# The last 64 keys of a slot in half-width values and quarter-array sums, and a new order of loads at the start, in a gated cross-attention block

## The chip, the cores and the metric

The kernel runs on one core of a Trainium2 chip (trn2). The metric is the device time of one execution in microseconds (us); lower is better. PE is TensorE, the matmul engine, PEld its weight loads; DVE is VectorE, ACT ScalarE, POOL GpSimd, SP SyncE. A line such as L891 is a line of the kernel before.

## The reference

One layer of a gated cross-attention block with a ternary feed-forward net. There are 16 batches, 224 rows of 512 in `x`, and 750 context keys of 384 in each; a mask leaves out part of the keys. There are 8 heads of 64, and gelu is the exact one.

```python
def attention(x, context, mask):          # x is layernormed first
    q = x @ W_q;  k = context @ W_k;  v = context @ W_v        # 8 heads of 64
    sim = einsum('bihd,bjhd->bhij', q, k) * 64 ** -0.5
    sim = where(mask[:, None, None, :], sim, -finfo.max)
    return einsum('bhij,bjhd->bihd', softmax(sim), v) @ W_o + b_o
def bitlinear(x, w, b):
    return act_quant(rmsnorm(x)) @ weight_quant(w).T + b       # 8 bits; -1, 0, 1
x = x + tanh(g_xattn[0]) * attention(layernorm(x), context, mask)
x = x + tanh(g_ffn[0]) * bitlinear(gelu(bitlinear(layernorm(x), w1, b1)), w2, b2)
```

`weight_quant` divides by the mean of |w| over the whole matrix, so no weight of w1 or w2 (each 1,048,576 values, 4.2 MB) can be rounded before all of them have been summed.

## The kernel before, in words

`order_batches` (L30) counts the keys that a batch attends to, sorts the batches by that count and gives each a slot. Slots 0 to 7 hold up to 192 keys, slots 8 to 15 up to 128 (`CAPS`). If all batches fit, `compact_path` (L709) runs, else `dense_path`; in the run shown it is `compact_path`. Only the kept keys are fetched, so a slot has one tile of 128 keys, and in slots 0 to 7 a second tile of 64, "the rest".

**One slot.** `select` (L797) builds six 0/1 masks on DVE (`ind`, L803), counts with them on PE which key goes to which place (`pi`, L810), and writes the key numbers and the mask for the scores (L819, L826). `gather` (L831) fetches these keys' context rows by an indirect DMA that POOL issues, 128 rows per tile, the second tile too. `context_pieces` (L854) turns the context on PE (`trans`, L867, six transposes of 128x128 in a slot with two tiles), makes the keys from it (`kp`, L876) and the values (`vp`, L891), one 128x512 projection of three matmuls for each tile. The second tile's values go into `v_rest`, a zeroed buffer of [128, 4, 2, 64] per parity of slot. Its 128 rows are the 64 keys twice: `place` repeats the numbers 128 to 191. Rows 0 to 63 hold the even head of a pair in the first 64 columns, rows 64 to 127 the odd head in the last 64, and the rest is zero, so that one full matmul adds the rest of both heads.

The x rows are fetched by `fetch` (L915), two tiles of 128 rows, layernormed by `norm` (L921: bn_stats and bn_aggr on DVE, then the power, the negated mean and the centring on POOL), turned (L951) and projected to queries (L972). `scores` (L1001) does, for four of the eight heads and half of the rows, four matmuls over 64 rows (L1011), the mask and minimum on DVE (L1025), exp on ACT (L1035), the reciprocal on DVE (L1044) and a multiply on POOL (L1045). `turn_probs` (L1055) transposes the probabilities into `pT`. `weighted` (L1079) sums them with the values: 16 half-width matmuls (64 output rows each) for the first tile (L1089), then, with a rest, four full ones with `v_rest` (L1100), all into two PSUM banks (index `a`); the heads of a pair lie in output rows 0 to 63 and 64 to 127. An fp32 matmul is two records of the trace.

**After attention**, pairs of 128-row tiles go through `residual` (L1134), `project` with `wo` (L1143, L1148), `normalise` (L1172), `up` (L1218), `gelu` (L1231) and `down` (L1264), with the FFN weights in fp8. These weights are made during slots 0 (w1) and 1 (w2): `load_weights` (L1299) brings eight chunks ("raw", 0.5 MB each), `sum_weights` (L1314) sums |w| on DVE and ACT by turns, `scale_weights` (L1329) adds up the sums with one PE matmul (`wtotp`), `round_weights` (L1350) rounds a chunk in three DVE passes into a bf16 tile of the tag `xq`, and `turn_weights` (L1359) turns it on PE. `evict` (L738) gives each copy out of PSUM to DVE or ACT, by running estimates of their load. PSUM has two wide tiles for scores, `av` and `hp`, and four banks for all else.

**Order.** Each slot is a loop pass (L1441): `merge` (L1389) interleaves three lists by their estimated costs in us: the attention of slot s, the preparation for later slots (`norm_pieces(s + 2)`, `gather(s + 2)`, `select(s + 3)`, context and queries of slot s + 1), and the weights (s < 2) or the FFN. Then the first two scores of slot s + 1 follow. Within that order a scheduler puts instructions into the engines' queues, each of which runs in order. Before the loop stands the start:

```python
    fetch(0)
    select(0)
    gather(0)
    norm(0, (0,))
    norm(0, (1,))
    fetch(1)
    select(1)
    gather(1)
    for piece in query_pieces(0) + context_pieces(0):
        piece[1]()
    fetch(2)
```

followed by `norm_pieces(1)`, `select(2)`, the eight loads of w1, `late_loads` (L220: b_o, b2, w_o and b1 on SP's queue, the biases broadcast to 128 partitions) and the first two scores of slot 0.

Of the kernel before, what the change touches and what calls it, by code (L numbers as in the profile page):

```python
# [29 lines left out]
def order_batches(ctx, tc, sh, mask, x, context):  # L30
# [44 lines left out]

    spread(spread_no, start, nc.gpsimd, nc.gpsimd)
# [15 lines left out]
    nc.gpsimd.tensor_copy(m, m8)  # L92

# [43 lines left out]
    nc.vector.tensor_copy(n_odd, odds)  # L137

# [19 lines left out]
def flamingo_gated_kernel(  # L158
# [61 lines left out]
    def late_loads():  # L220
        nc.sync.dma_start(sh.bo, b_o.partition_broadcast(P))
        nc.sync.dma_start(sh.b2, b2.partition_broadcast(P))
        nc.sync.dma_start(sh.wo, w_o.rearrange("(c p) i -> p c i", p=P))
        nc.sync.dma_start(sh.b1, b1.partition_broadcast(P))
# [4 lines left out]
    with few.Else():  # L229
        with ExitStack() as stage:  # L230
            late_loads()
# [477 lines left out]
def compact_path(ctx, tc, sh, x, context, out, late_loads):  # L709
# [74 lines left out]

    place = pa.tile([P, 256], BF16, name="place")
    numbers(place[:, :192], [[1, 192]], 0, 0)
    numbers(place[:, 192:], [[1, 64]], 128, 0)
    place_f = pa.tile([TQ, 320], BF16, name="place_f")
    numbers(place_f[:, :192], [[1, 192]], 0, 0)
    numbers(place_f[:, 192:], [[1, P]], 0, 0)  # L790
    first = pa.tile([P, B], F32, name="first")
    nc.gpsimd.tensor_scalar(first, sh.slots[:, 1, :], float(J), None, ALU.mult)

    live = [{} for _ in range(B + 1)]
    kctx = context.rearrange("b j c -> (b j) c")

    def select(s):  # L797

        st = live[s]
        nt = 2 if CAPS[s] > P else 1  # L800
        ind = pa.tile([TJ, NJ, 256], BF16, tag="ind", name=f"ind_{s}", bufs=1)
        for n in range(NJ):
            nc.vector.tensor_scalar(  # L803
                ind[:, n, : nt * P], place[:TJ, : nt * P], sh.upto[:, n, s : s + 1], None, ALU.is_ge
            )
        load["v"] += 6 * 200
        pi = gen([P, 2], F32, f"pi_{s}")
        for t in range(nt):
            for n in range(NJ):
                nc.tensor.matmul(  # L810
                    pi[:, t : t + 1],
                    lhsT=ind[:, n, t * P : (t + 1) * P],
# [6 lines left out]
        nc.vector.tensor_scalar(  # L819
            keys[:, :nt], pi[:, :nt], float(J - 1), first[:, s : s + 1], ALU.min, ALU.add  # L820
        )
# [5 lines left out]
            mb[:, :nm], place_f[:, :nm], sh.slots[:TQ, 0, s : s + 1], -FMAX, ALU.is_ge, ALU.mult  # L827
# [3 lines left out]
    def gather(s):  # L831
# [3 lines left out]
        for t in range(nt):  # L835
            nc.gpsimd.indirect_dma_start(
                out=kept[:, t, :],
                out_offset=None,
                in_=kctx,
                in_offset=bass.IndirectOffsetOnAxis(ap=st["keys"][:, t : t + 1], axis=0),  # L840
# [5 lines left out]


    v_rest = []
# [666 lines left out]
```

## Time and profile before

| what | value |
|---|---|
| time before, median of 3 runs | 785.88 us (785.7 to 787.6) |
| the profiled execution's own time | 788.52 us |
| its span, first to last instruction | 786.8 us |
| mean granted TensorE clock | 0.971 |
| busy PE / PEld / DVE / ACT / POOL | 696.5 / 448.0 / 508.5 / 392.1 / 367.7 us |
| DMA traffic | 59.53 MB in 87280 packets |
| vp (L891), both tiles, 144 records | 68.0 us |
| av of the rest (L1100), 64 records | 14.2 us |
| a chunk of w1 or w2 (0.5 MB), issue to landing | 4.9 us median |
| x tiles, issue to landing | 5.9 us median |

How to read the profile: a row of groups names the line, the engine, the operation, output and inputs, shapes and number of records, then the busy time in us, the mean ns of one, and the idle time just before them with what ended it. Records of matmuls overlap, so their means are longer than the distance between two of them. A row of busy time by stage gives the window, its length, busy us and records of PE, PEld, DVE, ACT and POOL, the granted clock, the DMA share and GB/s. A row of waits says which engine and line waited for which other engine and line, then total us, number of times and longest. The timeline gives start, length, engine, line and operation, and in brackets the idle time before it. The chain of waits follows the work that ended last back to the start.

### The profile page before, as it was taken

What the parts mean: (1) busy time and instruction counts of PE and PEld (TensorE: products, weight loads), DVE (VectorE), ACT (ScalarE), POOL (GpSimd) and SP (SyncE); (2) the same over time, 40 slices, a digit from 0 to 9 for tenths busy, and PEclk for the clock granted to TensorE, in tenths of its full rate; (3) what the DMA queues carried; (4) which work ended last, traced back from release to release, by engine and by line L of the source; (5) the groups of instructions that cost most, each with busy time, mean ns of one, the idle gap of its engine ahead of it and who ended that gap; (6) DMA issues with size and microseconds to landing.
All of it is one profiled execution on the core that took longest, in us unless ns stands there. A gap on an engine that the chain in (4) does not pass through costs nothing.

```text
span 786.8 us, 11011 instructions
## 1 busy us (share of the span) xinstructions
PE 696.5 (89%) x3790; PEld 448.0 (57%) x3790; DVE 508.5 (65%) x1281; ACT 392.1 (50%) x950; POOL 367.7 (47%) x478
## 2 busy tenths in 40 slices
PE   2588889899999899999989899989898999989762
PEld 2466666676566565665756476656574756543321
DVE  4366776667772955848568635575758577688960
ACT  0264937344563735628264674373737365455340
POOL 6834245746083451753728343655362525254331
PEclk9999999999999999999999989999999999999887
DMA  7913412101231401415032330141404031323331
GB/s 278 340 47 106 160 28 67 35 15 47 40 75 54 104 28 43 89 54 104 29 67 78 78 67 12 54 104 54 79 27 91 17 81 41 67 54 92 85 88 48
DMA packets 87280, 59.53 MB, mean 76 GB/s; under 512 B 75424, under 2 KB 75440, under 8 KB 87088
## 3 DMA queue, kind: packets, MB, share of 16 engines
q1 hardware_dynamic: 78960, 32.00, 17.6%
q0 software_dynamic: 8256, 26.75, 10.9%
q8 instruction: 32, 0.52, 0.3%
q14 instruction: 32, 0.26, 0.1%
HBM read 33.04 MB, written 7.34 MB: 51 GB/s over the span
## 4 chain that ended last, share of the span: by engine, by line
PE 63%; DVE 19%; ACT 5%; issue 4%; POOL 4%; DMA 2%; POOLq 0%; DVEq 0%; ACTq 0%; SPq 0%
PE qp L972 13%; PE fp L1264 10%; PE hp L1218 9%; PE vp L891 7%; PE kp L876 6%; PE op L1148 6%; DVE a L1241 5%; PE av L1089 3%; DVE h L1226 3%; PE ptp L1065 3%; PE sim L1011 3%; DVE hq L1244 2%; DVE ind L803 2%; PE av L1100 2%; DVE hq L1245 2%
## 5 line engine op out<-in xcount | busy, mean ns | idle before, releaser
L1045 POOL TENSOR_TENSOR p<-p,rec 112x768 f32<-112x768 f32 (+1 forms) x64 | 81.8, 1281 | 130.5 <-DVE rec L1044 61.7
L1226 DVE SCALAR_TENSOR_TENSOR h<-hp,c,b_bc 128x1024 f32<-128x1024 f32 x56 | 71.6, 1281 | 86.6 <-PE hp L1218 85.6
L1218 PE MATMUL hp<-w1T,xqT 128*128 128x512 fp8e4 x448 | 106.3, 384 | 8.9 <-DMA xqT<-xq 5.1
L1035 ACT ACTIVATE p<-p,nm 112x192 f32<-112x192 f32 (+1 forms) x256 | 106.7, 421 | 7.9 <-DVE nm L1025 7.0
L1264 PE MATMUL fp<-w2T,hqT 128*128 128x512 fp8e4 x448 | 103.7, 386 | 7.5 <-DMA hqT<-hq 7.5
L972 PE MATMUL qp<-xnT,wq_sb 128*128 128x224 f32 x512 | 106.4, 363 | 1.3 <-ACT xnT L747 1.1
L1148 PE MATMUL op<-wo_sb,xoT 128*128 128x512 f32 x224 | 106.2, 609 | 1.0 <-DVE keys L819 0.9
L972 PEld LDWEIGHTS qp<-xnT,wq_sb 128*128 128x128 f32 x512 | 98.7, 196 | 7.5 <-ACT xnT L747 1.9
L1025 DVE CUSTOM_DVE_ANT_0 p<-sim,mask 112x192 f32<-112x192 f32 (+1 forms) x256 | 70.3, 316 | 29.2 <-PE sim L1011 16.5
L1218 PEld LDWEIGHTS <-xqT 128*128 128x128 bf16 x448 | 43.8, 99 | 62.3 <-issue 13.8
L1241 DVE TENSOR_REDUCE a<-h 128x1 f32<-128x2048 f32 x28 | 63.9, 2281 | 22.6 <-ACT h L1238 22.6
L1264 PEld LDWEIGHTS <-hqT 128*128 128x128 bf16 x448 | 43.7, 99 | 59.6 <-DMA hqT<-hq 8.9
L1238 ACT ACTIVATE h<-h 128x2048 f32<-128x2048 f32 x28 | 53.5, 1912 | 42.2 <-DVE h L1226 24.4
L876 PE MATMUL kp<-ctxT,wk_sb 128*128 128x192 f32 (+1 forms) x384 | 65.5, 323 | 5.6 <-ACT xnT L747 3.6
L774 POOL DMA_INDIRECT x<-in_x_dram,token x28 | 33.1, 1182 | 77.2 <-PE ctxp L867 36.8
L891 PE MATMUL vp<-wv_sb,ctxT 128*128 128x512 f32 x144 | 68.0, 610 | 0.0
L876 PEld LDWEIGHTS kp<-ctxT,wk_sb 128*128 128x128 f32 x384 | 59.8, 207 | 13.3 <-ACT xnT L747 5.2
L747 ACT COPY qT<-qp 128x448 f32<-128x448 f32 x30 | 16.0, 532 | 94.8 <-PE qp L972 94.8
L1148 PEld LDWEIGHTS op<-wo_sb,xoT 128*128 128x128 f32 x224 | 40.4, 192 | 39.0 <-issue 35.6
L1011 PE MATMUL sim<-kT,qT 64*112 64x192 f32 (+1 forms) x512 | 55.2, 317 | 8.4 <-DVE nm L1025 7.4
L1250 ACT ACTIVATE sq<-h 128x2048 bf16<-128x2048 f32 x28 | 53.2, 1900 | 7.6 <-DMA hqT<-hq 3.9
L1011 PEld LDWEIGHTS sim<-kT,qT 64*112 64x112 f32 x512 | 37.9, 172 | 28.2 <-DVE nm L1025 11.6
(157 smaller groups left out, 1117.9 us busy)
## 6 DMA issues: line engine op xcount, KB each, us to landing
raw<-in_L_ffn_w_dram SPq DMA_DIRECT2D x16, 512.0 KB, 4.9
wq_sb<-in_L_xattn_W_q_dram SPq DMA_DIRECT2D x1, 1024.0 KB, 5.9
wo_sb<-in_L_xattn_W_o_dram SPq DMA_DIRECT2D x1, 1024.0 KB, 7.9
b_bc<-in_L_ffn_b_dram SPq DMA_DIRECT2D x1, 1024.0 KB, 11.1
wk_sb<-in_L_xattn_W_k_dram SPq DMA_DIRECT2D x1, 768.0 KB, 7.4
wv_sb<-in_L_xattn_W_v_dram SPq DMA_DIRECT2D x1, 768.0 KB, 8.9
x<-in_x_dram,token POOLq DMA_INDIRECT x28, 5.9
y<-in_x_dram,token POOLq DMA_INDIRECT x28, 3.4
```

Of the source, the lines that this page charges most:

```text
L876: nc.tensor.matmul(pk[:, p - p0, :], lhsT=sh.wk[:, c, p * P : (p + 1) * P], rhs=st["ctxT"][:, c, :cap], start=(c == 0), stop=(c == NC - 1),)
L891: nc.tensor.matmul(pv, lhsT=st["ctxT"][:, c, t * P : (t + 1) * P], rhs=sh.wv[:, c, :], start=(c == 0), stop=(c == NC - 1),)
L972: nc.tensor.matmul(pq[:, i, :], lhsT=sh.wq[:, d, (p + i) * P : (p + i + 1) * P], rhs=st["xnT"][:, d, :], start=(d == 0), stop=(d == ND - 1),)
L1011: nc.tensor.matmul(sim[:, j, i, :cap], lhsT=st["qT"][j * DH : (j + 1) * DH, p, q * TQ : (q + 1) * TQ], rhs=st["kT"][j * DH : (j + 1) * DH, ...
L1025: nc.vector.tensor_tensor_reduce(out=probs[:, h, :cap], in0=sim[:, j, i, :cap], in1=st["mask"][:, j * begin : j * begin + cap], scale=-(DH ...
L1035: nc.scalar.activation(probs[:, h, :cap], probs[:, h, :cap], AF.Exp, bias=nmax, scale=-1.0, accum_out=total[:TQ, h : h + 1],)
L1045: nc.gpsimd.tensor_tensor(probs[:, :, :cap], probs[:, :, :cap], rec[:TQ].unsqueeze(2).to_broadcast([TQ, 4, cap]), ALU.mult,)
L1148: nc.tensor.matmul(po, lhsT=xoT[:, d, at : at + P], rhs=sh.wo[:, d, :], start=(d == 0), stop=(d == ND - 1))
L1218: nc.tensor.matmul(ph[:, n, :], lhsT=f["xqT"][:, k * ND + d, :], rhs=w1T[:, d, at : at + NB], start=(d == 0), stop=(d == ND - 1),)
L1226: nc.vector.scalar_tensor_tensor(h[:, cols], ph.rearrange("t i n -> t (i n)"), f["c1", k], sh.b1[:, cols], ALU.mult, ALU.add)
L1241: nc.vector.tensor_reduce(amax[:, k : k + 1], h, AX.X, ALU.max, apply_absolute_value=True)
L1264: nc.tensor.matmul(po, lhsT=f["hqT", k][:, n, :], rhs=w2T[:, n, :], start=(n == 0), stop=(n == NF - 1))
```

## The change

What it does, in six parts:

- The rest is held once. `select` and `gather` handle 64 rows for the second tile (`rows_of`), `ctxT` is 192 wide, and the transposes of the second tile take 64 rows.
- The values of the rest (`values_rest`) are made in two halves of 64 output rows, even heads in rows 0 to 63 and odd heads in rows 64 to 127, each over 256 columns of `wv` read in runs of 64. `v_rest` becomes a dense rotating tile [128, 4, 64] that one copy fills; zeroed buffers and memsets go.
- In `weighted`, the rest is added by eight matmuls of 64 rows by 64 columns, and for `a` = 1 the two heads of a pair change places in the output rows (`a ^ j`). `late_loads` brings `wo` with the matching halves crossed.
- The number patterns `place`, `place_f` and `first` are made in `order_batches`, `first` on ACT.
- At the start, `norm_first` normalises each tile of x_0 by itself, with only the power on POOL; fetches of x_1 and x_2 and the gather of slot 1 are issued after that power, and the w1 loads right after the first of them. The w1 sums and scale come before the first scores; b_o, b1, b2 and the first half of `wo` get a one-element copy from the last sum, so that their loads wait for it.
- The w2 chunks are loaded and summed among the w1 rounding and turning (`weight_pieces`), the turn of a chunk comes two chunks after its rounding, and the `xq` tag has three buffers.

```diff
@@ order_batches @@
+    sh.place = const.tile([P, 192], BF16, name="place")
+    sh.place_f = const.tile([P, 320], BF16, name="place_f")
     spread(spread_no, start, nc.gpsimd, nc.gpsimd)
...
     nc.gpsimd.tensor_copy(m, m8)
+    numbers(sh.place, [[1, 192]], 0, 0)
+    numbers(sh.place_f[:, :192], [[1, 192]], 0, 0)
+    numbers(sh.place_f[:, 192:], [[1, P]], 0, 0)
...
     nc.vector.tensor_copy(n_odd, odds)
+
+    sh.first = const.tile([P, B], F32, name="first")
+    nc.scalar.activation(sh.first, sh.slots[:, 1, :], AF.Copy, scale=float(J))
@@ flamingo_gated_kernel @@
-    def late_loads():
+    def late_loads(crossed):
         nc.sync.dma_start(sh.bo, b_o.partition_broadcast(P))
         nc.sync.dma_start(sh.b2, b2.partition_broadcast(P))
-        nc.sync.dma_start(sh.wo, w_o.rearrange("(c p) i -> p c i", p=P))
+        by = w_o.rearrange("(c p) i -> p c i", p=P)
+        if crossed:
+
+            h = P // 2
+            nc.sync.dma_start(sh.wo[:, 0:2, :], by[:, 0:2, :])
+            nc.sync.dma_start(sh.wo[:h, 2:4, :], by[h:, 2:4, :])
+            nc.sync.dma_start(sh.wo[h:, 2:4, :], by[:h, 2:4, :])
+        else:
+            nc.sync.dma_start(sh.wo, by)
         nc.sync.dma_start(sh.b1, b1.partition_broadcast(P))
@@ compact_path @@
-    place = pa.tile([P, 256], BF16, name="place")
-    numbers(place[:, :192], [[1, 192]], 0, 0)
-    numbers(place[:, 192:], [[1, 64]], 128, 0)
-    place_f = pa.tile([TQ, 320], BF16, name="place_f")
-    numbers(place_f[:, :192], [[1, 192]], 0, 0)
-    numbers(place_f[:, 192:], [[1, P]], 0, 0)
-    first = pa.tile([P, B], F32, name="first")
-    nc.gpsimd.tensor_scalar(first, sh.slots[:, 1, :], float(J), None, ALU.mult)
-
+    def rows_of(s, t):
+        return min(CAPS[s] - t * P, P)
@@ select @@
-            nc.vector.tensor_scalar(
-                ind[:, n, : nt * P], place[:TJ, : nt * P], sh.upto[:, n, s : s + 1], None, ALU.is_ge
-            )
+            nc.vector.tensor_scalar(ind[:, n, :cap], sh.place[:TJ, :cap], sh.upto[:, n, s : s + 1], None, ALU.is_ge)
...
+            rows = rows_of(s, t)
             for n in range(NJ):
                 nc.tensor.matmul(
-                    pi[:, t : t + 1],
-                    lhsT=ind[:, n, t * P : (t + 1) * P],
+                    pi[:rows, t : t + 1],
+                    lhsT=ind[:, n, t * P : t * P + rows],
@@ after gather @@
-    v_rest = []
-    for i in range(2):
-        t = pa.tile([P, NP, 2, DH], F32, name=f"v_rest_{i}")
-        nc.gpsimd.memset(t, 0.0)
-        v_rest.append(t)
@@ context_pieces @@
             for c in range(c0, c1):
                 for t in range(nt):
+                    rows = rows_of(s, t)
                     nc.tensor.transpose(
-                        pt[:, c - c0, t * P : (t + 1) * P], st["ctx"][:, t, c * P : (c + 1) * P], ident
+                        pt[:, c - c0, t * P : t * P + rows],
+                        st["ctx"][:rows, t, c * P : (c + 1) * P],
+                        ident[:rows, :rows],
                     )
-            evict(st["ctxT"][:, c0:c1, : nt * P], pt, (c1 - c0) * nt * P)
+            evict(st["ctxT"][:, c0:c1, :cap], pt, (c1 - c0) * cap)
...
-        def values(t):
-            pv = gen([P, D], F32, f"vp_{s}_{t}")
+        def values():
+            pv = gen([P, D], F32, f"vp_{s}")
...
-            if t == 0:
-                evict(st["v"], pv, D)
-            else:
-                st["v_rest"] = v_rest[s % 2]
-                by = pv.rearrange("p (i j d) -> p i j d", j=2, d=DH)
+            evict(st["v"], pv, D)
+
+        def values_rest():
+
+            pv = gen([P, NP, DH], F32, f"vr_{s}")
+            for c in range(NC):
+                by = sh.wv[:, c, :].rearrange("p (i j d) -> p i j d", j=2, d=DH)
                 for j in range(2):
-                    rows = slice(j * DH, (j + 1) * DH)
-                    evict(st["v_rest"][rows, :, j, :], by[rows, :, j, :], D // 2)
+                    nc.tensor.matmul(
+                        pv[j * DH : (j + 1) * DH],
+                        lhsT=st["ctxT"][:, c, P:],
+                        rhs=by[:, :, j, :],
+                        start=(c == 0),
+                        stop=(c == NC - 1),
+                    )
+            st["v_rest"] = pa.tile([P, NP, DH], F32, tag="v_rest", name=f"v_rest_{s}", bufs=2)
+            evict(st["v_rest"], pv, D // 2)
@@ before slot_xnT @@
+    def norm_first(k):
+
+        xp = normed[0]
+        st = small(f"bs_x0_{k}", 6)
+        nc.vector.bn_stats(st, xp[:, k, :])
+        mv = small(f"mv_x0_{k}", 4)
+        nc.vector.bn_aggr(mv[:, :2], st)
+        rstd = small(f"rs_x0_{k}")
+        nc.vector.tensor_scalar(rstd[:, :1], mv[:, 1:2], EPS, None, ALU.add)
+        power = nc.gpsimd.tensor_tensor(rstd[:, :1], rstd[:, :1], sh.mhalf[:, :1], ALU.pow)
+        nc.vector.tensor_scalar(xp[:, k, :], xp[:, k, :], mv[:, 0:1], rstd[:, :1], ALU.subtract, ALU.mult)
+        return power.ins
@@ weighted @@
+                    rows = slice((a ^ j) * DH, ((a ^ j) + 1) * DH)
                     nc.tensor.matmul(
-                        by[j * DH : (j + 1) * DH, a, i, :],
+                        by[rows, a, i, :],
...
         if rest:
-            for a in range(2):
-                for i in range(2):
+
+            for i in range(2):
+                for a in range(2):
                     p = 2 * a + i
-                    nc.tensor.matmul(
-                        by[:, a, i, :],
-                        lhsT=st["v_rest"][:, p].rearrange("p j d -> p (j d)"),
-                        rhs=st["pT"][:, 8 + p, :],
-                        start=False,
-                        stop=(i == 1),
-                    )
+                    for j in range(2):
+                        keys = slice(j * DH, (j + 1) * DH)
+                        rows = slice((a ^ j) * DH, ((a ^ j) + 1) * DH)
+                        nc.tensor.matmul(
+                            by[rows, a, i, :],
+                            lhsT=st["v_rest"][keys, p, :],
+                            rhs=st["pT"][keys, 8 + p, :],
+                            start=False,
+                            stop=(i == 1),
+                        )
@@ normalise and round_weights @@
-            f["xq"] = pa.tile([P, 2, D], BF16, tag="xq", name=f"xq_{i}", bufs=2)
-            f["xqT"] = pa.tile([P, 2 * ND, P], BF16, tag="xq", name=f"xqT_{i}", bufs=2)
+            f["xq"] = pa.tile([P, 2, D], BF16, tag="xq", name=f"xq_{i}", bufs=3)
+            f["xqT"] = pa.tile([P, 2 * ND, P], BF16, tag="xq", name=f"xqT_{i}", bufs=3)
...
-        quantised[wi, c] = w16 = pa.tile([P, W], BF16, tag="xq", name=f"w16_{wi}_{c}", bufs=2)
+        quantised[wi, c] = w16 = pa.tile([P, W], BF16, tag="xq", name=f"w16_{wi}_{c}", bufs=3)
@@ weight_pieces @@
         p = []
         if wi == 1:
-            p += [(0.0, lambda c=c: load_weights(wi, c)) for c in range(NPC)]
-        p += [(0.4, lambda c=c: sum_weights(wi, c)) for c in range(NPC)]
-        p += [(0.1, lambda: scale_weights(wi))]
-        for c in range(NPC + 1):
+            p += [(0.0, lambda: scale_weights(1))]
+        for c in range(NPC + 2):
             if c < NPC:
-                p += [(0.0, lambda c=c: round_weights(wi, c))]
-            if c > 0:
-                p += [(0.6, lambda c=c: turn_weights(wi, c - 1))]
+                p += [(0.2, lambda c=c: round_weights(wi, c))]
+                if wi == 0:
+                    p += [(0.0, lambda c=c: load_weights(1, c))]
+            if c > 1:
+                p += [(0.6, lambda c=c: turn_weights(wi, c - 2))]
+                if wi == 0:
+                    p += [(0.0, lambda c=c: sum_weights(1, c - 2))]
         return p
@@ the start, after the functions of compact_path @@
     fetch(0)
     select(0)
     gather(0)
-    norm(0, (0,))
-    norm(0, (1,))
-    fetch(1)
     select(1)
-    gather(1)
+    norm_first(0)
+    with tc.issue_after(norm_first(1)):
+        fetch(1)
+        gather(1)
+        fetch(2)
+    late["stage"] = ExitStack()
+    late["raw"] = late["stage"].enter_context(tc.tile_pool(name="raw", bufs=1))
+    with tc.issue_after(load_weights(0, 0)):
+        for c in range(1, NPC):
+            load_weights(0, c)
     for piece in query_pieces(0) + context_pieces(0):
         piece[1]()
-    fetch(2)
     for _, piece in norm_pieces(1):
         piece()
     select(2)
-    late["stage"] = ExitStack()
-    late["raw"] = late["stage"].enter_context(tc.tile_pool(name="raw", bufs=1))
     for c in range(NPC):
-        load_weights(0, c)
-    late_loads()
+        sum_weights(0, c)
+    scale_weights(0)
+
+    for dst in (sh.wo[0:1, 0, 0:1], sh.bo[0:1, 0:1], sh.b1[0:1, 0:1], sh.b2[0:1, 0:1]):
+        nc.scalar.copy(dst, weight_sums[0][0:1, NPC - 1 : NPC])
+    late_loads(True)
     scores(0, 0)
     scores(0, 1)
```

## The prediction

> **What bounds the kernel now.** I read the page first, then busy time by stage, then who PE waited for, then the timeline of the start and of one slot.
>
> ```profile
> PE 696.5 (89%) x3790; PEld 448.0 (57%) x3790; DVE 508.5 (65%) x1281; ACT 392.1 (50%) x950; POOL 367.7 (47%) x478
> ...
> PE 63%; DVE 19%; ACT 5%; issue 4%; POOL 4%; DMA 2%; POOLq 0%; DVEq 0%; ACTq 0%; SPq 0%
> ```
>
> PE leads both in busy time and in the chain that ended last. By stage (length, then busy PE, PEld, DVE, ACT, POOL):
>
> ```profile
> 20.00:40.00 20.00, 10.85 (x46) 9.44 (x46) 6.38 (x15) 4.97 (x11) 15.60 (x21) 1.00 0.94 335
> ...
> 60.00:80.00 20.00, 15.81 (x100) 12.48 (x100) 14.46 (x37) 9.15 (x24) 7.01 (x9) 0.91 0.37 120
> ...
> 300.00:350.00 50.00, 49.17 (x251) 30.91 (x249) 33.39 (x78) 26.71 (x63) 24.55 (x31) 1.00 0.26 63
> ```
>
> There are three regimes. Until about 30 us PE hardly works while DMA is full (0.94). In slots 0 and 1 (to about 130 us) PE has holes. From there to 430 us it is busy 49 of 50 us, DVE 33: work taken from PE there is time. PE's longest wait and what stands behind it:
>
> ```profile
> PE xnp L951 <- POOL x L938: 14.4, 2, 12.9
> ```
>
> ```profile
> 12.09 1.25 POOL L774 DMA_INDIRECT x<-in_x_dram,token  x1 [0.18 <-issue]
> ...
> 25.94 0.77 POOL L938 TENSOR_SCALAR x<-x,ls_x,rs_x 128x512 f32<-128x512 f32 x1
> ...
> 28.58 0.76 POOL L938 TENSOR_SCALAR x<-x,ls_x,rs_x 128x512 f32<-128x512 f32 x1
> ```
>
> x is asked for at 12.1 us, lands at 20.6 (the first bn_stats starts there), and is centred at 29.3, because POOL issues a context gather between the small steps. The price of the edited matmuls (busy us, mean ns), and one slot of PE in order of time:
>
> ```profile
> L891 PE MATMUL vp<-wv_sb,ctxT 128*128 128x512 f32 x144 | 68.0, 610 | 0.0
> ...
> L1100 PE MATMUL av<-pT,v_rest 128*128 128x224 f32 x64 | 14.2, 366 | 0.0
> ```
>
> ```profile
> 195.75 2.62 PE L972 MATMUL qp<-xnT,wq_sb 128*128 128x224 f32 x13
> 198.30 1.73 PE L1089 MATMUL av<-pT,v 128*64 128x224 f32 x16
> 199.96 1.78 PE L1100 MATMUL av<-pT,v_rest 128*128 128x224 f32 x8
> ```
>
> Means overlap, so I price by spacing of starts: an fp32 matmul is two records, 429 ns apart at 512 columns, 189 at 224, 109 per transpose. The 16 half-width (64-column) records of L1089 take the time of 8 full ones of L1100: they run in pairs.
>
> **What the Trainium skill says.** "TensorEngine Tiling (Array Packing)", Key Properties: changing the tiling mode drains TensorE. The trace agrees and prices it: the last qp record starts at 198.02 and streams 0.19, yet av starts at 198.30; at every change between 128x128, 64-row and 64-column form the gap is 0.092 to 0.096 us, without a change 0.002. "TensorE: Matmul & The Clock Gate", Measured speedup vs the span model: matmuls in different tiles run together, each tile adding about 4 ns; av's pairs start 7 ns apart, four at once no run here shows. "DMA: Bandwidth & Descriptors", SWDGE vs HWDGE vs iDMA: GpSimd's and SP's transfers share the 16 engines, which go round-robin. The trace agrees: x needs 8.5 us from issue to landing when SP has just queued 2.5 MB (bo, b2, wo, b1), the later y loads 3.4.
>
> **The change part by part** (span 786.8).
>
> *Start.* Four iotas, `first` and two v_rest memsets leave POOL's way (9.4 to 11.9 us); the iotas now stand where POOL waited for perm (1.16 us idle), `first` on ACT ahead of mT, which it doesn't delay (both wait for PE). So x is issued at 9.4 and 10.9. bo, b2, b1 and half of wo are held until the last weight sum; 0.5 MB of wo goes early (1.3 us at 0.39 MB/us, the rate of the start). With 3.4 us plus half a microsecond of company x lands at 13.3 and 14.6. Then bn_stats 0.69, aggregate 0.15, add 0.15, POOL's power 0.59, and the centring on DVE. A DVE pass over 512 columns is 0.49 (L1194) to 1.07 (L1187); I take 0.6. Both halves are done at 18.1, against 29.3. PE's queries start at 19.4 instead of 31.1, and take 8 us as before (32 matmuls, which need 6.05 at the later spacing). That gain is not all kept. On DVE the first ctxT copy now stands behind bn_stats of x_3, which is fetched after x_1, ctx_1 and x_2, at about 25, and under the weights' 4.2 MB needs 6.5 us (33.5 to 39.9 before): ctxT at 33, keys to 37.3, values 2.6 + 1.4, selection 0.3. PE then has the weight total ahead of the first scores. Raws are issued at 16 to 21; with 2.1 MB of gathers, 6.3 MB at 0.36 MB/us end at 33.5, the last sum at 39: just hidden. First scores at 41.0 instead of 49.7: **-8.7** (bounds -4 and -11.5).
>
> *Slot 0* ran from 49.7 to 91.2 (the second scores of slot 1): 41.5, of which PE's work at the spacings above, mode changes included, is 32.3. Waits were listed at 1.1, 1.8, 2.2 and 1.6, and one 3.4 us window ran at half clock. Now w1's scale is known before the scores, so rounding fills DVE while it used to idle; three xq buffers and a turn two chunks later remove most waits. A new one comes: the first turned chunk stands in PE's queue behind rounding, which DVE does after eight score passes; queued behind it are slot 1's remaining transposes and keys. Scores +0.7, eight passes 2.4, three DVE passes of 0.65 and small ones put it at +7.3, where PE would be at +4: 3.3 us. Work 31.0 + 3.3: 34.3, **-7.2** (bounds -3, -10). w2's loads and sums move here (4.8 us each on DVE and ACT, hidden while DVE's 29 us stay under 34).
>
> *Slot 1*: 38.5 before. Work 31, a wait of 4 for w2's scale, 1.5 for slow clock: **-2** (0 to -5).
>
> *Values.* Three full matmuls were 6 x 0.429 = 2.57 us; now 12 records of 256 columns in pairs, 6 x 0.216 = 1.30: -1.28 a slot. The operand is read in runs of 64; no row shows that: bounds 1.3 and 2.6, I take 1.3, as the bytes per row are the same. *Weighted rest*: 8 x 0.189 = 1.51; now 16 quarter records. Four at once would be 0.76, pairs 1.51, one by one 3.02; I take 0.94[...]. *Transposes*: three of 128 become 64 columns, -0.16. *Selection*: the 64-column bf16 weight loads were 25 ns each; the Trainium skill ("TensorE: Matmul & The Clock Gate", Weight-path perf modes and LDWEIGHTS) gives fast load only to 128 columns, and columns/1.2 ns otherwise, 53 as an estimate: up to +0.17; no run shows it. *Mode changes*: in the order of instructions on PE there are 59 more in all (44 around the 64-row transposes, some 16 around the new values, 12 around selection, fewer between scores): +5.5 us.
>
> For slots 2 to 15 (contexts 3 to 7, weighted 2 to 7): -5 x 1.28 - 6 x 0.57 - 5 x 0.16 + 45 x 0.094 + 0.7 = **-5.3**. Evictions and selection get cheaper on DVE, ACT and POOL; none bounds there, so nothing. Slots 8 to 15 only change order, and the tail from 707 us not at all: 0, with 3 either way.
>
> Sum -8.7 - 7.2 - 2 - 5.3 = -23.2, span 763.6. The profiled execution took 788.5 for 786.8, the median is 785.9; so the median should be 762.7, say **762**; own range 751 to 772.
>
> **Rivals.** *Loads replace x as the wait.* Everything held now comes after the raws, and PE waits for the last sum. For it: DMA is 0.94 full from 20 to 40 us, and several DVE steps stand behind landings. Against: 2 MB less traffic ahead. If the last raw lands as in before (41), first scores come at 48: 769 to 771.
> *Narrow tiles don't pay.* Strided values at half rate and quarters in pairs: the 1.28 and 0.57 go in all eight slots (14.8), mode changes stay: 777. For it: neither form is in the trace. Against: av's pairs.
> *Slower: quarters run one by one*, as the four matmuls cross row and column halves of two banks. Then the rest costs 3.02 a slot, another 8 x 1.51 = 12.1 on the last case: 789. It decides once less than 12 is kept of start and slots 0 and 1. Against it: the 7 ns pairs in both directions, rows (L1011) and columns (L1089).
>
> **Numbers.** Main case 0.71 (762), loads 0.13 (770), narrow tiles 0.11 (777), one by one 0.05 (789). The range takes the main case's edges, the loads and the nearer half of narrow tiles: 750 to 777. About 0.3% (2.4 us) can be told from no change: faster 0.93, same 0.02, slower 0.05.
>
> **What would show it.** Queries near 19 and first scores near 41; a long PE wait for a rounded chunk in slot 0; 12 values records in 1.5 us, 16 quarter records in 1.0; 0.09 us on each side of the short transposes; slots 3 to 6 about 1 us shorter. I am wrong if first scores come after 46, or quarter records start 189 ns apart.

## The result, and the profile after

The changed kernel took 779.72 us (median of 4 runs, 778.34 to 781.09) against 786.26 before on the same chip: a ratio of 0.9905, interval 0.9889 to 0.9921. It is faster, by 0.95% where 3% was forecast, and outside the range of 750 to 777. The profiled execution took 781.03 us for a span of 779.2; the forecast for the span was 763.6, so 15.6 us of gain are missing.

The page after, the two lines that were shown of before:

```profile
PE 698.1 (90%) x3902; PEld 446.6 (57%) x3902; DVE 514.6 (66%) x1293; ACT 387.4 (50%) x947; POOL 370.9 (48%) x468
...
PE 67%; DVE 16%; ACT 5%; issue 4%; DMA 3%; POOL 2%; DVEq 0%; POOLq 0%; ACTq 0%; SPq 0%
```

PE was to lose work, yet it is busy 1.6 us longer. The busy time by stage says why (the clock is the third number from the end):

```profile
20.00:40.00 20.00, 13.45 (x53) 12.31 (x53) 8.18 (x13) 5.16 (x11) 9.49 (x12) 0.85 0.77 281
60.00:80.00 20.00, 16.71 (x112) 12.56 (x110) 19.27 (x46) 16.81 (x42) 11.01 (x11) 0.91 0.58 179
300.00:350.00 50.00, 47.41 (x251) 29.41 (x250) 29.08 (x78) 24.95 (x59) 25.17 (x30) 0.93 0.26 63
```

From 300 to 350 us the clock was 1.00 before and is 0.93 now; from 60 to 80 DVE, 14.5 of 20 us busy before, is now full at 19.3. The waits of PE have moved as well. x's wait of 12.9 us is down to 4.8, and two others have grown: the kernel before had 7.4 us of the first kind and none of the second.

```profile
PE sim L1045 <- DVE nm L1059: 12.6, 9, 2.7
...
PE kp L890 <- issue: 6.0, 1, 6.0
```

The matmuls themselves became as cheap as forecast. One slot of PE in order of time, and then the start of the next slot's third scores:

```profile
233.62 1.74 PE L1124 MATMUL av<-pT,v 128*64 128x224 f32 x16
235.29 0.99 PE L1139 MATMUL av<-pT,v_rest 64*64 64x224 f32 x16
236.21 5.35 PE L1257 MATMUL hp<-w1T,xqT 128*128 128x512 fp8e4 x24
241.49 1.51 PE L916 MATMUL vr<-wv_sb,ctxT 128*64 128x256 f32 x12
242.94 1.56 PE L1045 MATMUL sim<-kT,qT 64*112 64x192 f32 x16
...
245.50 3.70 PE L1187 MATMUL op<-wo_sb,xoT 128*128 128x512 f32 x8
...
251.67 1.06 PE L1045 MATMUL sim<-kT,qT 64*112 64x192 f32 x8 [1.72 <-DVE nm L1059]
253.53 0.98 PE L1045 MATMUL sim<-kT,qT 64*112 64x192 f32 x2 [0.80 <-DVE nm L1059]
254.44 1.11 PE L985 MATMUL xnp<-ident,x 128*128 128x128 f32 x4
```

The 16 quarter records take 0.99 us where 8 full ones took 1.78, and the 12 half-width values 1.51 where 6 full ones took 2.74. (Sixteen records are eight matmuls; that holds for the first tile's half-width sums too, which "The kernel before, in words" calls 16 matmuls.) The quarters start four at a time, 6 to 7 ns apart within a four, and 0.19 to 0.24 us from one four to the next. But then PE waits for DVE's score passes, and after the wait everything takes twice as long: two score records 0.98 us (0.58 before), four transposes of x 1.11 (0.66). PE runs at half clock, for 10.24 us here.

Where the time went, from the first scores and the last weighted record of slots 2 and 7 in each trace. The third and fourth columns are experiments that are told below (one half of the change each), the others repairs of the changed kernel:

| us | before | changed | arrays alone | start alone | costs 5 to 8 | combined |
|---|---|---|---|---|---|---|
| first scores at | 49.7 | 47.0 | 47.7 | 48.0 | 46.4 | 40.0 |
| until the end of slot 2 | 164.1 | 153.5 | 167.8 | 159.0 | 153.3 | 143.9 |
| slots 3 to 7 | 230.4 | 236.1 | 238.0 | 230.4 | 225.3 | 225.3 |
| the rest | 392.3 | 389.5 | 390.1 | 393.5 | 392.1 | 393.3 |
| span | 786.8 | 779.2 | 795.9 | 782.8 | 770.7 | 762.6 |

The change gains 10.6 us until slot 2, loses 5.8 in slots 3 to 7, and gains 2.8 in the rest. Within slots 3 to 7 the loss is not even: slots 3 and 4 are 1.3 us shorter each, as the cheaper matmuls let expect; slots 5, 6 and 7 are 2.5, 2.7 and 3.2 us longer.

### The profile page after: what moved, and what is told of

Its sections match the earlier page's. It is cut to its first block, busy times and chain, and to the rows that moved or that the text cites. A ratio compares the mean times of both kernels' runs of the same rounds, so it can differ in the third digit from the quotient of the medians.

```text
span 779.2 us, 11250 instructions
## 1 busy us (share of the span) xinstructions
PE 698.1 (90%) x3902; PEld 446.6 (57%) x3902; DVE 514.6 (66%) x1293; ACT 387.4 (50%) x947; POOL 370.9 (48%) x468
## 3 DMA queue, kind: packets, MB, share of 16 engines
q0 software_dynamic: 8128, 25.96, 10.6%
## 4 chain that ended last, share of the span: by engine, by line
PE 67%; DVE 16%; ACT 5%; issue 4%; DMA 3%; POOL 2%; DVEq 0%; POOLq 0%; ACTq 0%; SPq 0%
PE qp L1006 12%; PE hp L1257 10%; PE fp L1303 10%; PE kp L890 8%; PE op L1187 7%; DVE a L1280 4%; PE vp L905 4%; PE av L1124 4%; PE sim L1045 3%; DVE hq L1283 3%; DVE h L1265 3%; PE ptp L1099 3%; DMA raw<-in_L_ffn_w_dram 2%; ACT h L1277 1%; ACT p L1069 1%
## 5 line engine op out<-in xcount | busy, mean ns | idle before, releaser
L1257 PE MATMUL hp<-w1T,xqT 128*128 128x512 fp8e4 x448 | 108.7, 389 | 8.0 <-DMA xqT<-xq 5.1
L890 PE MATMUL kp<-ctxT,wk_sb 128*128 128x192 f32 (+1 forms) x384 | 68.3, 330 | 7.9 <-issue 6.0
L890 PEld LDWEIGHTS kp<-ctxT,wk_sb 128*128 128x128 f32 x384 | 62.5, 211 | 15.5 <-issue 8.9
L1045 PE MATMUL sim<-kT,qT 64*112 64x192 f32 (+1 forms) x512 | 56.8, 327 | 12.7 <-DVE nm L1059 12.6
L791 POOL DMA_INDIRECT x<-in_x_dram,token x28 | 33.8, 1206 | 59.6 <-PE xnp L985 42.0
L764 ACT COPY kT<-kp 128x256 f32<-128x256 f32 (+2 forms) x43 | 17.4, 405 | 79.3 <-PE kp L890 71.3
```

The costliest lines, as they stand in the source:

```text
L890: nc.tensor.matmul(pk[:, p - p0, :], lhsT=sh.wk[:, c, p * P : (p + 1) * P], rhs=st["ctxT"][:, c, :cap], start=(c == 0), stop=(c == NC - 1),)
L1045: nc.tensor.matmul(sim[:, j, i, :cap], lhsT=st["qT"][j * DH : (j + 1) * DH, p, q * TQ : (q + 1) * TQ], rhs=st["kT"][j * DH : (j + 1) * DH, ...
L1257: nc.tensor.matmul(ph[:, n, :], lhsT=f["xqT"][:, k * ND + d, :], rhs=w1T[:, d, at : at + NB], start=(d == 0), stop=(d == ND - 1),)
```

## The experiments

**Where slots 3 to 7 lose.** The diff also changed two numbers that the prediction didn't price: the planned costs in `context_pieces`, from 2.6 and 2.6 to 1.5 and 0.8. `merge` orders the work by them. Before, PE's order at the end of a slot was up projection, the rest's values, up projection, first scores, two of eight records of an output projection, second scores:

```profile
252.78 2.74 PE L891 MATMUL vp<-wv_sb,ctxT 128*128 128x512 f32 x6
255.35 1.89 PE L1218 MATMUL hp<-w1T,xqT 128*128 128x512 fp8e4 x8
257.17 0.91 PE L1011 MATMUL sim<-kT,qT 64*112 64x192 f32 x8
...
258.65 1.02 PE L1148 MATMUL op<-wo_sb,xoT 128*128 128x512 f32 x2
259.60 0.91 PE L1011 MATMUL sim<-kT,qT 64*112 64x192 f32 x8
260.44 2.84 PE L1148 MATMUL op<-wo_sb,xoT 128*128 128x512 f32 x6
...
264.60 0.58 PE L1011 MATMUL sim<-kT,qT 64*112 64x192 f32 x2 [0.66 <-DVE k L1159]
```

Now all up projections come first, then the rest's values, both scores together, the eight records of the output projection and, after a few transposes, the third scores. They need a wide PSUM tile that DVE's passes free, and DVE has no hole there from 241.6 to 256.1 us (a pass of 1.28 for `h`, two reductions of 4.47 together, two rounding passes of 1.29 and 1.28, their casts, the score passes). So the first experiment put back the numbers alone.

```diff
-        pieces.append((1.5, values))
+        pieces.append((2.6, values))
         if nt > 1:
-            pieces.append((0.8, values_rest))
+            pieces.append((2.6, values_rest))
```

> The changed kernel with one thing different: the two values pieces carry 2.6 and 2.6 as planned costs, as before the change, in place of 1.5 and 0.8. The instructions are the same, only their order on the engines differs: in slots 4 to 6 an up projection stands between the values and the second scores of the next slot wait behind half of the output projection, as before. Theory A (the gain of the narrow values is lost because the new planned costs bring the third scores of a slot to PE ahead of DVE's passes, and each such wait of 1.7 to 2.7 us is followed by 6.8 to 10.2 us at half clock): the waits of the scores in slots 5 to 7 and their half-clock stretches go, 3 x (about 2 + 4), and some is lost elsewhere: about 767 us. Rival B (slots 4 to 7 are bound by DVE whatever the order, or the clock falls because of the narrow tiles themselves): the waits only move, 777 to 781 us.

Measured: 775.67 us, ratio 0.9856 (0.9824 to 0.9887), span 775.0. The waits and half-clock stretches of slots 5 to 7 went, and slots 3 to 7 took 223.8 us instead of 236.1; but slots 0 to 2 ended at 157.4 instead of 153.5. Theory A held where it was made, and the total missed because the same numbers order the contexts of all slots: slots 1 and 2 took 4.1 us longer than in the changed kernel. Giving the old numbers to the contexts of slots 5 to 8 only:

```diff
-        pieces.append((1.5, values))
+        pieces.append((2.6 if 5 <= s <= 8 else 1.5, values))
         if nt > 1:
-            pieces.append((0.8, values_rest))
+            pieces.append((2.6 if 5 <= s <= 8 else 0.8, values_rest))
```

> The changed kernel with the old planned costs of the values (2.6 each) for the contexts of slots 5 to 8 only; slots 0 to 4 and 9 to 15 keep the new ones. With old costs everywhere slots 4 to 7 took 187.1 us (from the last weighted record of slot 4 to that of slot 8) against 196.6, but slot 1 lost 3.9. Theory A: both halves are separate, so this order gives the 9.5 back and loses nothing in slot 1: a span of 769 to 771. Rival: the half clock falls by the place on its grid, and moves to other waits: 774 or more.

Measured: 771.12 us, ratio 0.9785 (0.9756 to 0.9814), span 770.7, as A expected. Slots 3 to 7 took 225.3, 5.1 less than before. Slot 2 ended at 153.3, so the early slots kept what they had gained. The order alone is worth 8.5 us of span.

**The wait or the clock?** A wait of 1.7 us can't cost 4 by itself. This run left every order as it is and put useless work into the three waits.

```diff
+            if c0 == 2 and s in (6, 7, 8):
+                bank = gen([P, NB], F32, f"ctxp_{s}_{c0}")
+                pt = bank[:, :cap].rearrange("p (c r) -> p c r", c=1)
+                for k in range(6):
+                    nc.tensor.matmul(
+                        bank[:, 256:448], lhsT=ident, rhs=sh.wk[:, 0, :192], start=(k == 0), stop=(k == 5)
+                    )
...
```

> The changed kernel, every engine's order as it is, with six useless 192-column fp32 matmuls (12 records of 163 ns, 1.96 us) put on PE ahead of the last transposes of the contexts of slots 6, 7 and 8: they stand just before the scores that wait 1.7, 1.7 and 2.7 us in slots 5, 6 and 7. Their result goes to an unused part of a PSUM bank; nothing of the computation is left out. Theory A (a stretch of about 3.4 us in which PE is busy half of the time or less halves its clock): the waits are filled, the three half-clock stretches of 10.2, 6.8 and 6.8 us go, and the added work costs next to nothing: 3 to 5 us each, a span of 767 to 770. Rival B (the clock follows the narrow tiles or the load, not the waits): the half-clock stretches stay, a span of 779 to 785.

Measured: 770.72 us, ratio 0.9791 (0.9764 to 0.9818), span 769.2. The kernel with 36 more records on PE has a span 10 us shorter. In slot 5 the third scores start at 251.5 us, where they started at 251.7, so the wait was filled and not shortened. The busy time in stretches of 3.41 us, first of the changed kernel, then with the filled waits (PE stands just behind the length, the clock is the third number from the end):

```profile
248.88:252.29 3.41, 1.69 (x15) 1.20 (x13) 3.41 (x10) 3.40 (x10) 2.08 (x2) 1.00 0.27 53
252.29:255.71 3.42, 2.62 (x11) 1.39 (x8) 3.42 (x20) 3.42 (x10) 3.23 (x3) 0.50 1.04 249
255.71:259.12 3.41, 3.41 (x11) 1.94 (x12) 1.42 (x8) 3.22 (x14) 2.98 (x7) 0.50 0.92 217
259.12:262.53 3.41, 3.41 (x11) 2.59 (x10) 0.00 (x0) 0.00 (x0) 0.39 (x1) 0.50 0.00 0
262.53:265.95 3.42, 3.42 (x11) 1.75 (x10) 0.18 (x1) 1.40 (x4) 1.18 (x1) 1.00 0.00 0
```

```profile
248.71:252.13 3.42, 3.42 (x27) 3.02 (x25) 3.42 (x10) 3.41 (x10) 2.06 (x2) 1.00 0.27 51
252.13:255.54 3.41, 2.47 (x15) 1.52 (x13) 3.41 (x20) 3.41 (x10) 3.23 (x3) 1.00 1.04 242
255.54:258.95 3.41, 3.41 (x21) 2.33 (x20) 1.44 (x8) 3.41 (x15) 2.98 (x7) 1.00 0.96 225
```

A stretch with PE busy 1.69 of 3.41 us is followed by half clock, here until PE had been full for two stretches at the lower clock; filled, the clock stays at 1.00. Slots 3 to 7 took 226.1 us here, 10.0 less than in the changed kernel: what they had lost was the clock. The Trainium skill ("TensorE: Matmul & The Clock Gate", Part 1: The HAM clock gate) describes a free-running window of 3413 ns with half rate after an idle one. The trace agrees on the window: the half-clock stretches of the changed kernel start at multiples of 3.41 us from each other, and last 3.41, 6.83 or 10.24, the very last apart. It differs on the trigger: PE need not be idle, half busy was enough. Of the changed kernel's twelve half-clock stretches eleven follow one in which PE was busy half of the time or less, and one follows 1.96 of 3.41 us (50.91 to 54.32). The limit isn't sharp in these records: 2.57 of 3.41 us was followed by half clock in the run with the start alone (51.11 to 54.52), and 1.56 was not in the run with old costs everywhere and all repairs (386.60 to 390.01).

**The start.** The first turned context stood on DVE behind the statistics of x_3's first tile, whose gather was issued at 26.4 us and landed at 33.7, and behind a weight sum of 1.20 us that began at 33.3. (The expectation below calls it x_1's second half; x_1's gathers landed at 24.8 and 26.6.) Timeline of the changed kernel, DVE and then PE:

```profile
34.42 0.68 DVE L950 BATCH_NORM_STATS2 bs_x<-x 128x6 f32<-128x512 f32 x1
35.02 0.54 DVE L761 COPY ctxT<-ctxp 128x384 f32<-128x384 f32 x1
```

```profile
28.28 1.40 PE L879 MATMUL ctxp<-ident,ctx 128*128 128x128 f32 x6
35.66 6.60 PE L890 MATMUL kp<-ctxT,wk_sb 128*128 128x192 f32 x24 [5.98 <-issue]
42.10 2.74 PE L905 MATMUL vp<-wv_sb,ctxT 128*128 128x512 f32 x6
```

```diff
+            if s == 0:
+                nc.scalar.copy(st["ctxT"][:, c0:c1, :cap], pt)
+            else:
-            evict(st["ctxT"][:, c0:c1, :cap], pt, (c1 - c0) * cap)
+                evict(st["ctxT"][:, c0:c1, :cap], pt, (c1 - c0) * cap)
```

> The changed kernel with the copies of slot 0's turned context put on ACT, so that the first no longer stands on DVE behind the statistics of the second half of x_1. Theory A (this copy alone holds PE from 29.7 to 35.7 us and so causes the half clock from 33.8 to 40.7): keys start near 30.5, no half clock there, first scores near 41 instead of 47, and the time falls by 3 to 6 us, to about 775. Rival (the last weight sum, after the raws that land until 36, or the first gathers of slot 1 take its place): first scores at 44 or later and less than 2 us gained, 778 or more.

Measured: 774.61 us, ratio 0.9860 (0.9806 to 0.9915), span 773.6, 5.6 less. Keys start at 31.3 and take 4.17 us instead of 6.60, first scores come at 40.7:

```profile
31.30 4.17 PE L893 MATMUL kp<-ctxT,wk_sb 128*128 128x192 f32 x24 [0.80 <-ACT ctxT L885]
...
40.34 0.38 PE L1374 MATMUL wtotp<-wtot,ones 128*128 128x1 f32 x2 [0.34 <-DVE wtot L1372]
```

So one copy of 0.54 us in the wrong queue cost 6.4 us at the first scores, the half clock behind it included. Of these, 4.2 were left at the end of slot 2. The rival, the loads, shows as the 0.34 us for the weight total: they are just hidden, as forecast. In time the gain is less certain than in the trace: one of the four executions took 780.57 us, and the interval overlaps that of the changed kernel (0.9889 to 0.9921).

**Slot 0.** The held b_o lands at 51.5 us, so POOL scales it and b2 then, ahead of the first probabilities:

```profile
51.51 2.62 POOL L1502 TENSOR_SCALAR bo_bc<-bo_bc,tgates 128x512 f32<-128x512 f32 x1 [1.25 <-DMA bo_bc<-in_L_xattn_b_o_dram]
54.13 2.35 POOL L1503 TENSOR_SCALAR b_bc<-b_bc,tgates 128x512 f32<-128x512 f32 x1
56.46 3.50 POOL L1079 TENSOR_TENSOR p<-p,rec 112x768 f32<-112x768 f32 x2
```

Before, these two ran at 31.1 and 37.5 us, 1.6 us each, and nobody waited for them. The first edit queued them behind slot 3's gathers:

```diff
...
-                nc.gpsimd.tensor_scalar(sh.bo, sh.bo, sh.tgates[:, 0:1], None, ALU.mult)
-                nc.gpsimd.tensor_scalar(sh.b2, sh.b2, sh.tgates[:, 1:2], None, ALU.mult)
+                with tc.issue_after(last_gather[0].ins):
+                    nc.gpsimd.tensor_scalar(sh.bo, sh.bo, sh.tgates[:, 0:1], None, ALU.mult)
+                    nc.gpsimd.tensor_scalar(sh.b2, sh.b2, sh.tgates[:, 1:2], None, ALU.mult)
```

> The changed kernel with POOL's two multiplies of b_o and b2 by the gates queued behind the gathers of slot 3's context, after the first probabilities. Theory A (held loads put these 5 us of POOL at 51.5 us, ahead of slot 0's probabilities, which pushes the gathers and the third probabilities; PE then waits 3.3 us at 67.4, and the half clock from 71.4 follows): PE's wait near 67 falls under 1 us, slot 0 is shorter by 4 to 5 us, time about 775. Rival (DVE's rounding sets slot 0, POOL only stands beside it): the wait stays or turns into a wait for the rounded chunk, 778 to 780.

Measured: 781.76 us, ratio 0.9930 (0.9905 to 0.9956), span 779.4: no gain. In POOL's order these gathers stand just ahead of slot 0's third probabilities, so the two multiplies still came first, at 68.6 to 72.5, and PE's wait grew to 6.5 us. So the edit left what it was to remove, and says nothing on Theory A. It showed something else: slot 0 ended 3.7 us later than in the changed kernel, yet by the end of slot 5 both stood at 289.6. The waits in slot 5 are 1.72 and 0.95 us (1.72 and 0.80 in the changed kernel), but no half clock followed:

```profile
252.42:255.84 3.42, 1.70 (x11) 0.87 (x9) 3.42 (x9) 3.41 (x8) 1.55 (x1) 1.00 0.09 18
255.84:259.25 3.41, 2.46 (x17) 1.50 (x17) 3.41 (x19) 3.41 (x9) 3.19 (x3) 1.00 1.07 224
```

Busy 1.70 of 3.42 us here, 1.69 of 3.41 above, and the opposite outcome: slot 5 took 49.5 us here and 53.7 there. Near half, the same wait costs some 4 us or nothing, and what decides is not shown: in both runs the wait of 1.72 us lies within one stretch. The mended edit queues the multiplies behind slot 1's first probabilities:

```diff
...
-                nc.gpsimd.tensor_scalar(sh.bo, sh.bo, sh.tgates[:, 0:1], None, ALU.mult)
-                nc.gpsimd.tensor_scalar(sh.b2, sh.b2, sh.tgates[:, 1:2], None, ALU.mult)
+                with tc.issue_after(shares[4].ins):
+                    nc.gpsimd.tensor_scalar(sh.bo, sh.bo, sh.tgates[:, 0:1], None, ALU.mult)
+                    nc.gpsimd.tensor_scalar(sh.b2, sh.b2, sh.tgates[:, 1:2], None, ALU.mult)
```

> The changed kernel with the two multiplies of b_o and b2 queued on POOL behind the first probabilities of slot 1, so that nothing of them stands ahead of any of slot 0's. Theory A (these multiplies, held back with their loads, push slot 0's third probabilities): POOL is free for these 4 to 5 us earlier, they then start as soon as DVE has their reciprocal near 67 us, PE's wait for them falls from 3.3 to about 1.3 us, and the span is 2 to 4 us shorter, 775 to 777. Rival B (POOL's and DVE's work is stretched in any case while DVE rounds, so the same wait comes from another POOL instruction): the wait stays at 3 us or more, the span within 1 us of 779.2.

Measured: PE's longest wait for probabilities is 1.1 us instead of 3.3, slot 0's last weighted record starts at 81.5 instead of 84.0, and the span is 775.4. In time, 778.21 us and a ratio of 0.9898 (0.9859 to 0.9937) can't be told from the changed kernel's 0.9905. The mechanism is shown by the trace, its worth in time is not.

**Both halves of the change by themselves.** First the arrays in the kernel before (rest held once, values in halves, quarters, crossed `wo`, new planned costs; start, loads, order of weights and buffers as before):

```diff
-        pieces += [(2.6, lambda t=t: values(t)) for t in range(nt)]
+        pieces.append((1.5, values))
+        if nt > 1:
+            pieces.append((0.8, values_rest))
...
-    late_loads()
+    late_loads(True)
```

> The kernel before with only the edits of the rest: 64 rows held once, values in two halves, quarters of the array, crossed wo, the new planned costs; start, loads, weight order and buffers as before. Theory A (prices as forecast, and most of it lost in slots 4 to 7 to waits and half clock): 2 to 3 us gained in slots 0 to 3 beyond the start, about 8 lost in slots 4 to 7 against what they give, time 781 to 785, with the waits of the scores of 1.7 to 2.7 us in slots 5 to 7. Rival (narrow tiles lose by themselves): slots 2 to 4 longer than before, 788 or more.

Measured: 797.66 us, ratio 1.0123 (1.0091 to 1.0154), span 795.9. Both expectations missed. The signs of the rival came: over 788 us, and slots 2 to 4 together 0.8 us longer than before. Its reason didn't: the narrow records were as cheap as in the changed kernel (12.1 us busy for all of the rest's values, 7.9 for its sums, in both), and within slots 2 to 4 PE ran at half clock for 10.2 us where it was 3.4, which alone costs 3.4 us. Slots 3 to 7 lose by the scores' waits as in the changed kernel, and slots 0 to 2 end 3.7 us later:

```profile
PE sim L1031 <- DVE nm L1045: 12.7, 9, 2.7
...
PE wp L1392 <- DVE w L1381: 8.3, 2, 6.9
...
PE wp L1396 <- DVE w L1381: 5.1, 1, 5.1
```

The wait for the first rounded chunk of w1, 2.2 us before, became 6.9, and half clock followed it for 6.8. PE's order shows one reason: before, 3.3 us of queries and 0.9 of scores stood ahead of that chunk's wait, and now the queries stand behind it. Then the start and the weights alone:

```diff
-    norm(0, (0,))
-    norm(0, (1,))
-    fetch(1)
+    norm_first(0)
+    with tc.issue_after(norm_first(1)):
+        fetch(1)
+        gather(1)
+        fetch(2)
...
-        nc.gpsimd.memset(t, 0.0)
+        nc.vector.memset(t, 0.0)
```

> The changed kernel without its array part: selection, gather, transposes, values, v_rest and weighted sums as before the change (the zeroing of v_rest on DVE, so that it stays out of x's way); start, held loads, weight order and buffers as changed. The array part alone made the kernel before 1.2% slower. Additive: this one is then faster than the changed kernel by as much, a span of 768 to 771. Theory A (in slots 0 and 1 DVE's rounding is the bound with either kind of values, once the weights' order is changed, and slots 3 to 15 then run as before, 622.7 us after the 157 to 160 of the old planned costs): 779 to 783.

Measured: 784.14 us, ratio 0.9965 (0.9951 to 0.9979), span 782.8, near what Theory A expected. The halves don't add: +1.2% and -0.35% give -0.95%. Until slot 2 the start gains 5.1 us with the old arrays and 14.3 with the new (167.8 to 153.5). That fits the arrays' long waits for rounding (6.9 and 5.1 us alone, 1.6 and 3.6 with the new start), but no run takes these waits away by themselves.

**All repairs together.** Old costs everywhere, the copy on ACT and the first, unlucky place of the scaling:

> The changed kernel with all three: old planned costs of the values, slot 0's turned context copied on ACT, and the scaling of the biases queued late. If the three causes are separate, gains add: 779.7 - 13 - 5 - 4.5 = about 757 us. If they overlap (the same DVE or POOL backlog behind all of them), 763 or more.

Measured: 768.92 us, ratio 0.9777 (0.9747 to 0.9807), span 767.1: the second case of the expectation, a smaller gain than the sum, with the old costs in the early slots again. With the costs by slot and the mended scaling:

> The changed kernel with slot 0's turned context copied on ACT, the old planned costs for the contexts of slots 5 to 8 and the scaling of the biases behind slot 1's first probabilities. If gains add, 779.2 - 5.6 - 9.5 - 3 = a span of 761 us, time about 763. If the start's gain is lost again in slot 0: 766 or more.

Measured: 764.59 us, ratio 0.9698 (0.9665 to 0.9732), span 762.6. The gains nearly add: 5.6, 8.5 and 3.8 us of span alone, 16.6 together. Then the second tile's selection, gather and transposes at full width again:

```diff
     def rows_of(s, t):
-        return min(CAPS[s] - t * P, P)
+        return P
...
```

> The combined version (turned context of slot 0 on ACT, old planned costs for the contexts of slots 5 to 8, late scaling) with selection, gather and transposes of the second tile at 128 rows again, the 64 keys twice, as before the change; the narrow values and quarters stay. Theory A (the 64-row transposes cost more in mode changes than they save: a slot's six take 0.97 + 0.47 us in the changed kernel, 0.64 + 0.38 before): some 0.4 us a slot in seven slots, 3 us less, a span near 759.5. Rival (DVE, POOL and DMA pay for the doubled rows, or a wait takes it): 762 to 765.

Measured: 762.21 us, ratio 0.9665 (0.9629 to 0.9701), span 761.2. The intervals of this run and the last overlap, and the span lies between the two expectations. The trace says where 0.4 us a slot went in slots 3 to 5: PE's waits at 193, 241 and 292 us, the first for DVE's key numbers, the others for ACT's copies, 1.40, 0.99 and 1.06 us long, became 2.10, 1.62 and 1.68. There PE waited for at least what it saved. Last, useless matmuls in the two long waits of the tail:

```diff
+        if i == NTOK // 2 - 1 and k == 0 and g == 0:
+            keep_busy(20, pairs[i - 1]["xqT"], f"fill_up_{i}")
...
+        if i == NTOK // 2 - 1 and k == 0:
+            keep_busy(28, f["xqT"], f"fill_down_{i}")
```

> The full-width version of the combined kernel (span 761.2) with useless matmuls on PE in the last two waits for DMA transposes: 20 of 512 columns (4.3 us) ahead of the last pair's first up projection, where PE waits 5.1 us, and 28 (6.0 us) ahead of its down projection, where PE waits 6.8. Nothing of the computation is left out. Theory A (these waits halve the clock of what follows): the 16 up records then take 3.6 us instead of 5.9 and the last 32 down records 7.0 instead of 9.9, some 5 us less, a span of 755 to 757. Rival B: the clock stays low or the fill delays the transposes, 761 or more.

Measured: 762.72 us, ratio 0.9692 (0.9661 to 0.9723), span 761.0. The time is the rival's. The clock stayed full until the last down projection had ended, and it gained nothing: PE now waits for the next transposes instead (2.4, 1.4 and 2.7 us), and the last down projection starts at 737.3 us where it started at 737.6. In this tail the end waits for the transposes and not for PE, so half clock cost nothing.

## Why the prediction was wrong, step by step

**The start** (-8.7 forecast, -2.7 measured). x was issued at 9.8, normalised at 19.0, and queries started at 20.7: forecast 9.4, 18.1 and 19.4. The step named the right copy behind the right statistics. Of the 6 us that are missing, 2.7 are the copy's delay (keys start at 35.7, forecast 33; a weight sum stood ahead too) and 2.3 the keys at half clock (6.6 us instead of 4.3); 0.6 is a slip of the sum, whose terms lead to 41.6 and not 41.0. The step that failed is that a wait of PE was priced by its length, without the half clock behind it (33.8 to 40.7), and that its length was put too short. First scores after 46 were the prediction's own sign of being wrong, and they came at 47.0. With the copy elsewhere they come at 40.0 to 40.7. That this is near the 41.0 of the forecast is in part luck, as keys then start at 31.3 and not at 33.

**Slot 0** (-7.2 forecast, -1.8 measured: 39.7 us from the first scores to slot 1's second, 34.3 forecast). The wait for the rounded chunk was put at 3.3 and was 1.6. Put at nothing were the scaling of the biases, which the held loads drag behind them (3.3 us of wait), and two stretches of half clock (6.8 us long, 3.4 us lost). The change holds loads back, and the forecast followed the loads, but not the instructions that read them.

**Slot 1** (-2 forecast, -1.1 measured). The wait for w2's scale was put at 4; it was 1.1, with 3.6 more for w2's first rounded chunk, and the clock took 3.4 us where 1.5 was put.

**The arrays** (-5.3 forecast for slots 2 to 15, where the terms as written give -5.7; -2.1 measured). The prices held. From the first start to the next instruction, less the mode change, the quarters took 0.83 us (0.94 taken; four at once, as they run, was priced at 0.76), the values 1.35 (1.30). The short transposes cost what the mode changes were priced at: 0.97 and 0.47 us against 0.64 and 0.38. The 64-column weight loads of the selection came 28 to 32 ns apart, not 53. With the old order in slots 5 to 8, slots 3 to 7 gain 5.1. What failed is "work taken from PE there is time", read from 49 busy us of 50. Inside each slot there is a stretch in which DVE has no hole (14.5 us in slot 5), and what PE is given to do beside it is set by the planned costs, which changed. The sum took the order of work as fixed.

**The rivals.** Quarters run together and the columns in runs of 64 are read at full rate, so "narrow tiles don't pay" and "one by one" fell. "Loads replace x" fell too. The point at which the last rival decides, less than 12 us kept of the start and slots 0 and 1, was reached (5.6 of 17.9 kept), but by the copy, the scaling and the clock, and without slow quarters.

**The repaired kernel.** That its span of 762.6 lies near the forecast 763.6 is luck in part. Slot 0 gives 4.2 us of the 7.2 forecast, and everything from slot 2 on 9.1 where 5.3 was forecast.

## What to carry to other kernels

Before a saving on the leading engine is counted, look inside the stage for stretches in which another engine has no hole: a saving there can turn into a wait, and here a wait that left PE about half busy over 3.4 us could double the price of what followed. Planned costs that order the work are part of a change, and shorter matmuls with truthful costs can bring the wrong order; compare the order around the next wait, not the sum. A load that is held back takes its readers with it, into the queues of engines that had been idle when they ran before.

## What was not expected of the hardware

- Half clock comes in stretches of 3.41 us and its multiples, mostly after stretches in which PE was half busy or less. Near the limit it is open what decides: one and the same wait of 1.72 us was followed by 10.24 us of it, or by none.
- POOL and DVE can hold each other up. The Trainium skill ("GPSIMD Engine Reference", 8. Key points) says that they share their SBUF interfaces and contend when a DVE instruction runs in a 2-port mode or has two SBUF inputs; no run here tells the mode of these passes, but the trace shows a price. POOL's multiply of 112x768 took 1.47 us at 210.6 us of the changed kernel, where DVE was idle, and 4.89 us at 54.3 us in the run with the scaling behind slot 3's gathers, while DVE rounded weights. In the changed kernel a rounding pass of DVE took 0.67 us at 52.3, and 1.95 at 56.7 us while POOL multiplied.
